# A planned delta-rule and mixture-of-experts layer: the experts' first products of the last three groups move to the projections' two PSUM banks, and the hand-over of the last chunks uses a second bank

## The chip, the core and the metric

The kernel runs on one core of a Trainium2 chip. The time is the device time of one execution in microseconds, and the figure given for a kernel is the median of its runs. A core has five engines that run beside each other, each with an instruction queue of its own that is worked through strictly in order: TensorE (PE, with its weight loads as PEld), VectorE (DVE), ScalarE (ACT), GpSimd (POOL) and SyncE (SP, which only issues transfers here). TensorE writes into PSUM, which is cut into eight banks of 512 fp32 words per partition. The kernel uses all eight.

## The reference

The input is `x` of shape (4, 1024, 128). All arithmetic is fp32. First comes an attention layer by the gated delta rule, then a layer norm; then a block with ordinary attention over the batch and a mixture of eight experts, then a layer norm. Cut to what matters:

```
# 1. delta rule: 16 heads of 8, causal over 1024 steps
q, k, v = silu(conv4(silu(x W + b)))          # q, k normalised per token over all 128 channels
a, b    = sigmoid(x Wa + ba), sigmoid(x Wb + bb)
S_t = a_t S_{t-1} - a_t b_t (S_{t-1} k_t) k_t^T + b_t v_t k_t^T
o_t = q_t S_t
x   = layernorm(x + o Wo + bo)
# 2. block: attention among the 4 places "t" of each token row, then experts
qkv = src @ in_proj_w.T + in_proj_b
x   = ln(src + softmax(q k) v @ out_w.T + out_b, ln1)
probs = softmax(tok @ gate_w.T + gate_b);  topv, topi = top_k(probs, 2)
for e in range(8):
    h = relu(tok @ w1[e].T + b1[e]) @ w2[e].T + b2[e]      # 128 -> 512 -> 128
    moe_out += combine[:, e:e+1] * h
x   = layernorm(x + ln(x + moe_out, ln2))
```

## The kernel before

The 1024 steps are cut into eight chunks of 128 (`NCHUNK`). Each chunk `c` goes through a fixed series of stages: `project` (inputs transposed, q, k, v and the two gates), `prepare` (convolution, the products k.k, a small triangular solve), `recur` (the recurrence, sixteen blocks of eight steps, each a multiply and a sum on VectorE twice over), `output` (what q reads from the states), `attend` and `attended` (the block's attention, layer norms, the gate and the ranks of the tokens), and then `experts`, which takes the chunks in the groups `(0, 1), (2, 3), (4, 5), (6,), (7,)`.

`experts` scatters every token twice into a buffer in HBM sorted by expert (L1555, an indirect transfer issued by POOL), reads it back in tiles of 128 rows, four at a time (`xl`), transposes them (L1571, bank `ph`), scales them on ScalarE (L1573, `xlT`), and then works tile by tile. One tile has one expert: its weights, 514 KB, are fetched by SP into one of three buffers `w_e` (L1586); four matmuls of 128x128 make the hidden layer in `ps_h` (L1596); four activations on ScalarE (L1605) add the bias and apply relu; four matmuls (L1609) make the result in the bank `pm`. A copy (L1617) and a transfer take four tiles to HBM (`ys`). When a group is done, POOL gathers each token's two rows (L1627), VectorE sums them, and two layer norms finish the chunk. There are 23 tiles in each group of two chunks and 15 in each group of one, 99 in all; in the text below they are counted 0 to 98, so that group (4, 5) has tiles 46 to 68, group (6,) tiles 69 to 83 and group (7,) tiles 84 to 98.

PSUM is handed out by tag, one bank for each buffer of a tag: `pa` has two banks (projections and convolutions), and `pk` (k.k), `su` (the states), `po` (output), `pc` (attend and attended), `ph` (transposed rows and hidden layer) and `pm` have one each. All instructions that touch one bank follow each other, whichever part of it they touch.

The order of the instructions is not the order of the program text. The program is recorded once; `forward` then plays it through with a list scheduler that has a table of costs (`price`), of delays between engines (`HOP`, row the waiting engine, column the one waited for), and of the transfers' rate; and `put_in_order` fixes the order that comes out, engine by engine. The rank of an instruction is the length of what follows it plus a number from `LEAD`: one row for each stage in the order of the text, one number for each sixty instructions of it. Where the plan leaves TensorE idle for more than `FILL_MIN`, `fillers` puts idle matmuls (L612, of the identity matrix) that keep its clock up; they write into whichever bank is free.

Of the kernel before, what the change touches and what calls it, by code (L numbers as in the profile page):

```python
# [84 lines left out]
class Slots:  # L85
# [33 lines left out]


HOP = (
    (0.0, 0.054, 0.053, 0.054, 0.05, 0.044),
    (0.038, 0.0, 0.033, 0.034, 0.04, 0.03),
    (0.037, 0.035, 0.0, 0.04, 0.04, 0.05),
    (0.09, 0.08, 0.063, 0.0, 0.06, 0.07),
    (0.031, 0.028, 0.026, 0.027, 0.0, 0.017),
)

OVERLAP = (0.0, 0.083, 0.11, 0.043, 0.0)

# [1 line left out]

PIECE = 60
LEAD = (
    (-596, -698,),
    (-695,),
    (1215, 1142,),
    (-239,),
    (-326,),
    (42, 327,),  # L140
    (-717, -154,),
    (-605, -1049,),
    (-810,),
    (-141, -914,),
    (-468,),
    (847, 645,),
    (142, 371,),
    (832, -867,),
    (-1488,),
    (-525, 14,),  # L150
    (21,),
    (154, 573,),
    (-536, 239,),
    (150, -335,),
    (-139, 302, 1084, 833, 618, 867, 306, -62, 535,),
    (-103,),
    (-319, 358,),
    (21,),
    (822, 1113,),
    (325, 133,),  # L160
    (-330, -211,),
    (-341,),
    (-499, -431,),
    (-273,),
    (809, 430,),
    (21, 79,),
    (510, -110,),
    (-99, 422, 15, 260, -43, 347, -211, 876, 125,),
    (-488,),
    (97, -532,),  # L170
    (-438,),
    (334, 1061,),
    (82, -55,),
    (-748, -468,),
    (-347,),
    (-566, -206,),
    (-890,),
    (673, 244,),
    (-525, -84,),
    (-74, -848,),  # L180
    (330, -102, -426, -699, -279, -40, -524, 453, 218,),
    (-566,),
    (129, -1199,),
    (-377, -137,),
    (-533, 514,),
    (378, 91, 339, 237, 165, 545,),
    (172,),
    (-80, 3,),
    (-409, -393, 106, 565, -698, 771,),
)  # L190
WINDOW, DOWN, UP = 3.413, 0.39, 0.77
FILL, FILL_MIN, FILLER = 0.7, 0.5, 0.225
TABLES = {"Silu": 1, "Sigmoid": 2, "Exp": 3}


# [221 lines left out]
def forward(units, rank):  # L417


    q = Queue(units, [u.preds for u in units], rank)  # L420
    begin_, end_ = [0.0] * len(units), [0.0] * len(units)
    order = [[] for _ in range(5)]
    size, cols, dma, pool, dve, table = None, [0.0] * 4, 0.0, 0.0, 0.0, 0
    slow, window, busy, carry, holes = True, 0, 0.0, 0.0, []
    for _ in units:
        now, e, k = q.take()
        u = units[k]
        begin = now
        if e == PE_:
            own, col = u.tile  # L430
            if size not in (None, own):
                begin = max(begin, max(cols)) + 0.1
            begin = max(begin, cols[col] if own[1] == 32 else max(cols))
            idle = max(cols + [q.free[e]])
            share = FILL * (begin - idle) if begin - idle > FILL_MIN else 0.0
            if share:
                holes.append((len(order[0]), idle, begin))
            spent = 0.0
            while True:
                t = idle + spent if share else begin  # L440
# [24 lines left out]
            end = begin + cost + u.long - u.cost  # L465
        elif u.bytes:
            dma = max(begin + u.cost + 0.2, dma) + u.bytes / 265e3
            end = dma + 1.4
            q.free[e] = begin + u.cost
        else:  # L470
            alone = u.kind in ("TensorTensor", "TensorScalarPtr", "TensorCopy")
            if e == DVE_ and alone and not any(u.psum):
                begin = max(begin, pool)
            if e == POOL_ and alone:
                begin = max(begin, dve)
            if e == ACT_ and u.table and u.table != table:
                begin += 1.28
                table = u.table
            end = begin + u.long
            q.free[e] = begin + u.cost  # L480
            if e == POOL_ and u.kind != "DMACopy":
                pool = end - 0.05
            if e == DVE_ and alone and not any(u.psum):
                dve = end - 0.05
        order[e].append(k)
        begin_[k], end_[k] = begin, end
        transfer = u.kind == "DMACopy"
        for s in u.succs:
            v = units[s]
            if v.engine != e or transfer:  # L490
                q.release(s, end + HOP[v.engine][5 if transfer else e])
            else:
                q.release(s, end if k in v.waits and e != PE_ else begin)
    return begin_, end_, order, holes


# [98 lines left out]
def delta_moe_kernel(  # L595
# [680 lines left out]
    def attend(c):  # L1276
# [25 lines left out]
        x1Tf = x1T.rearrange("p s t -> p (s t)")  # L1302

        def projected(i):
            ps = psum.tile([P, B, T], F32, tag="pc", name=f"ps_qkv{c}_{i}", bufs=1)
            nc.tensor.matmul(
                ps,
                lhsT=in_w[:, i * C : (i + 1) * C],
                rhs=x1Tf,
                start=True,  # L1310
                stop=True,
            )
            return ps
# [45 lines left out]
    def attended(c):  # L1359
# [1 line left out]
        x1, sc, v = scored.pop(c)  # L1361
        cxs = []
        for s in range(B):
            ps = psum.tile([P, B, T], F32, tag="pc", name=f"ps_a{c}_{s}", bufs=1)
            for f in range(2):
                nc.tensor.matmul(  # L1366
                    ps[:, :, f * T // 2 : (f + 1) * T // 2],
                    lhsT=spread[:, s, f],
                    rhs=sc,
                    start=True,  # L1370
                    stop=True,
                )
            cx = tile2k(f"cx{c}_{s}", "prod", 6)
            nc.vector.tensor_tensor(cx, ps, v, MUL)
            cxs.append(cx)
# [114 lines left out]
    def experts(group):  # L1490
# [71 lines left out]
        for i0 in range(0, nt, Q):  # L1562
# [18 lines left out]
            for i in range(m):  # L1581
                e = nc.sync.value_load(
                    expert_of[0:1, i0 + i : i0 + i + 1], min_val=0, max_val=E - 1
                )
                w = pl.tile([P, WP], F32, tag="w_e", name=f"w{g0}_{i0 + i}", bufs=3)
                nc.sync.dma_start(  # L1586
                    w, d["wp"][bass.ds(e, 1)].rearrange("o p f -> (o p) f")
                )
                w1 = w[:, 0:F]
                w2 = w[:, F : F + NF * C].rearrange("p (f c) -> p f c", f=NF)  # L1590
                b1 = w[:, F + NF * C : F + NF * C + NF]
                ps = psum.tile(
                    [P, NF, P], F32, tag="ph", name=f"ps_h{g0}_{i0 + i}", bufs=1
                )
                for f in range(NF):
                    nc.tensor.matmul(  # L1596
                        ps[:, f, :],
                        lhsT=w1[:, f * P : (f + 1) * P],
                        rhs=xlT[:, i, :],
                        start=True,  # L1600
                        stop=True,
                    )
                h = pl.tile([P, NF, P], F32, tag="h", name=f"h{g0}_{i0 + i}", bufs=2)
                for f in range(NF):
                    nc.scalar.activation(  # L1605
                        h[:, f, :], ps[:, f, :], AF.Relu, bias=b1[:, f : f + 1]
                    )
                for f in range(NF):
                    nc.tensor.matmul(  # L1609
                        ps_y[:, i, :],  # L1610
                        lhsT=h[:, f, :],
                        rhs=w2[:, f, :],
                        start=(f == 0),
                        stop=(f == NF - 1),
                    )
# [223 lines left out]
```

## Time and profile before

| | us |
|---|---|
| median of three runs (lowest, highest) | 833.56 (831.26, 834.96) |
| time of the profiled execution | 832.78 |
| its span, from the first instruction to the last | 831.1 |
| PE, DVE, POOL, ACT busy in the span | 699.4, 564.6, 475.4, 412.8 |
| last block of the last recurrence starts its last multiply | 565 |
| first matmul of tile 46, the first of group (4, 5) | 620.9 |
| last matmul of tile 98 | 802.5 |

A busy time is the sum of an engine's instructions in the one profiled execution. Matmuls overlap each other and their ends are modelled, so TensorE counts as busy for longer than the array works. The kernel has two halves with different limits: up to about 565 us the recurrence runs, and after it only what follows it is left. So shares over the whole span say little, and each part has to be read in its own stretch. Lines named below (L1596 and so on) are those of the kernel before.

### The profile page before, as it was taken

What the parts mean: (1) busy time and instruction counts of PE and PEld (TensorE: products, weight loads), DVE (VectorE), ACT (ScalarE), POOL (GpSimd) and SP (SyncE); (2) the same over time, 40 slices, a digit from 0 to 9 for tenths busy, and PEclk for the clock granted to TensorE, in tenths of its full rate; (3) what the DMA queues carried; (4) which work ended last, traced back from release to release, by engine and by line L of the source; (5) the groups of instructions that cost most, each with busy time, mean ns of one, the idle gap of its engine ahead of it and who ended that gap; (6) DMA issues with size and microseconds to landing.
All of it is one profiled execution on the core that took longest, in us unless ns stands there. A gap on an engine that the chain in (4) does not pass through costs nothing. (4 is left out here: it accounts for less than half of the span.)

```text
span 831.1 us, 15634 instructions
## 1 busy us (share of the span) xinstructions
PE 699.4 (84%) x5000; PEld 516.5 (62%) x5000; DVE 564.6 (68%) x1742; ACT 412.8 (50%) x1163; POOL 475.4 (57%) x656
## 2 busy tenths in 40 slices
PE   8989797889985988999889888799898999977750
PEld 5555545456553673667677577577477878777640
DVE  2167897898977998989899888987426351531303
ACT  5246362555653435486456435455325565465531
POOL 3534339849646748846746987653778621662213
PEclk9999999999997999999989999999899999999995
DMA  7642244252425245378458648568268688788741
GB/s 204 172 136 85 90 128 130 79 178 79 127 89 156 75 148 171 104 218 264 147 175 279 192 124 249 151 193 264 87 203 231 215 231 256 229 243 258 210 124 29
DMA packets 120070, 139.67 MB, mean 168 GB/s; under 512 B 9517, under 2 KB 90933, under 8 KB 119989
## 3 DMA queue, kind: packets, MB, share of 16 engines
q1 hardware_dynamic: 115893, 130.29, 52.0%
q0 software_dynamic: 4096, 8.40, 3.6%
q8 instruction: 39, 0.64, 0.3%
q14 instruction: 42, 0.34, 0.1%
HBM read 99.53 MB, written 39.12 MB: 167 GB/s over the span
## 5 line engine op out<-in xcount | busy, mean ns | idle before, releaser
L1605 ACT ACTIVATE h<-ps_ph,w_e 128x128 f32<-128x128 f32 x396 | 115.0, 368 | 91.2 <-PE ps_ph L1596 46.8
L1609 PE MATMUL ps_pm<-w_e,h 128*128 128x128 f32 x792 | 134.8, 296 | 19.9 <-ACT h L1605 18.6
L1609 PEld LDWEIGHTS ps_pm<-w_e,h 128*128 128x128 f32 x792 | 110.7, 193 | 39.8 <-ACT h L1605 34.9
L1596 PE MATMUL ps_ph<-xlT,w_e 128*128 128x128 f32 x792 | 116.8, 287 | 8.2 <-ACT xlT L1573 4.4
L1596 PEld LDWEIGHTS ps_ph<-xlT,w_e 128*128 128x128 f32 x792 | 101.1, 196 | 21.2 <-ACT xlT L1573 9.3
L897 PE MATMUL ps_pa<-z,diag 128*128 128x512 f32 x192 | 94.3, 620 | 7.8 <-ACT conv L906 3.0
L1627 POOL DMA_INDIRECT yg<-dr_ys,rows_at x64 | 62.2, 972 | 56.1 <-DMA dr_ys<-yl 26.9
L1555 POOL DMA_INDIRECT sorted<-x,rows_at x64 | 63.3, 989 | 49.9 <-DVE rows_at L1551 20.1
L1107 ACT ACTIVATE p<-ps_su,g_block 128x32 f32<-128x32 f32 x127 | 40.3, 317 | 98.4 <-DVE ps_su L1101 95.9
L1201 POOL TENSOR_TENSOR out_work<-sc__0_704,qg_r 128x512 f32<-128x512 f32 x64 | 73.4, 1165 | 14.3 <-PE ps_po L1205 5.7
L1633 DVE SCALAR_TENSOR_TENSOR acc<-yg,g2x,acc 128x128 f32<-128x128 f32 x64 | 24.0, 379 | 72.1 <-DMA yg<-dr_ys,rows_at 71.9
L1110 DVE TENSOR_TENSOR p<-ps_su,kd_r 128x256 f32<-128x256 f32 x127 | 53.1, 418 | 19.2 <-ACT p L1107 18.8
L897 PEld LDWEIGHTS ps_pa<-z,diag 128*128 128x128 f32 x192 | 33.9, 194 | 43.7 <-issue 30.3
L1101 DVE TENSOR_REDUCE ps_su<-z 128x32 f32<-128x288 f32 x128 | 58.1, 454 | 1.9
L1095 DVE TENSOR_TENSOR z<-ps_su,wt 128x256 f32<-128x256 f32 x128 | 53.4, 417 | 8.5 <-ACT su_out L1133 3.9
L1116 DVE TENSOR_REDUCE ps_su<-p 128x32 f32<-128x288 f32 x127 | 57.5, 453 | 1.6
L1173 POOL TENSOR_TENSOR out_work<-uc,q_r 128x192 f32<-128x192 f32 (+3 forms) x64 | 51.0, 827 | 12.3 <-DMA uc<-dr_su_back 11.8
L1219 POOL TENSOR_TENSOR out_work<-k_r,qu 128x128 f32<-128x128 f32 (+6 forms) x64 | 50.7, 818 | 7.8 <-DVE o L1227 5.3
L1086 ACT COPY z<-x 128x32 f32<-128x32 f32 x128 | 30.7, 245 | 38.7 <-DVE ps_su L1101 38.3
L940 POOL TENSOR_TENSOR work<-conv 128x320 f32<-128x320 f32 (+6 forms) x56 | 36.0, 666 | 22.4 <-DVE x L1035 19.5
L1035 DVE TENSOR_REDUCE x<-work 128x128 f32<-128x256 f32 (+6 forms) x56 | 45.5, 812 | 1.2 <-ACT work L1026 0.3
L1252 ACT ACTIVATE acc<-acc,le_nm,le_rs 128x128 f32<-128x128 f32 x64 | 28.1, 496 | 34.0 <-DVE le_nm L1250 34.0
(209 smaller groups left out, 1481.6 us busy)
## 6 DMA issues: line engine op xcount, KB each, us to landing
w_e<-in_wp SPq DMA_DIRECT2D x99, 514.0 KB, 4.7
dr_bounce<-conv SPq DMA_DIRECT2D x24, 256.0 KB, 2.4
xl<-sorted SPq DMA_DIRECT2D x21, 256.0 KB, 3.2
dr_ys<-yl SPq DMA_DIRECT2D x21, 256.0 KB, 5.0
kd_r<-dr_bounce SPq DMA_DIRECT2D x16, 256.0 KB, 3.1
work<-dr_bounce SPq DMA_DIRECT2D x16, 256.0 KB, 4.5
dr_su_back<-su_out SPq DMA_DIRECT2D x8, 512.0 KB
sorted<-yl SPq DMA_DIRECT2D x10, 256.0 KB, 4.3
```

Of the source, the lines that this page charges most:

```text
L897: nc.tensor.matmul(ps, lhsT=diag[:, i, j, :], rhs=z[:, i, :, j : j + T], start=(j == 0), stop=(j == KC - 1),)
L1095: nc.vector.tensor_tensor(z1n[:, :, :, 0:DH], s[:, :, None, :].to_broadcast([P, HD, J, DH]), wt[n // HALF][:, None, here_cut, :].to_broadc ...
L1101: nc.vector.tensor_reduce(u, z1n, AX.X, ADD)
L1110: nc.vector.tensor_tensor(p3[:, :, :, 0:J], u[:, :, None, :].to_broadcast([P, HD, DH, J]), ks[:, None, :, cut].to_broadcast([P, HD, DH, J] ...
L1116: nc.vector.tensor_reduce(ring[:, (n + 1) % (2 * RING), 0 : HD * DH].rearrange("p (d e) -> p d e", e=DH), p3, AX.X, ADD,)
L1173: gp.tensor_tensor(t[:, :, row_of(j) - r0 : row_of(j + 1) - r0], uv[:, :, 0 : j + 1], qv[:, :, j : j + 1].to_broadcast([P, BN, j + 1]), MUL,)
L1201: gp.tensor_tensor(t, sv[:, :, :, d_ : d_ + 1].to_broadcast([P, B, NB, J]), gv, MUL)
L1555: gp.indirect_dma_start(views[(i * 2 + g) * B + s][0 : nt * P, :], bass.IndirectOffsetOnAxis(ap=rows_at[:, g, s : s + 1], axis=0), x2[:, s ...
L1596: nc.tensor.matmul(ps[:, f, :], lhsT=w1[:, f * P : (f + 1) * P], rhs=xlT[:, i, :], start=True, stop=True,)
L1605: nc.scalar.activation(h[:, f, :], ps[:, f, :], AF.Relu, bias=b1[:, f : f + 1])
L1609: nc.tensor.matmul(ps_y[:, i, :], lhsT=h[:, f, :], rhs=w2[:, f, :], start=(f == 0), stop=(f == NF - 1),)
L1627: gp.indirect_dma_start(yg[:, s, :], None, ys[0 : nt * P, :], bass.IndirectOffsetOnAxis(ap=rows_at[:, g, s : s + 1], axis=0),)
```

## The change

Three sets of banks are changed. The hidden layers of the groups from chunk 4 on take turns in the two banks of `pa`, which no projection uses any more by then, instead of sharing the one bank `ph` with the transposes. For chunks 6 and 7 the products for v and q, and every second of the four products of attention, go to `pk`; the others stay in `pc`. The planner gets a longer delay from ScalarE to TensorE (0.053 to 0.1 us) and a table `SELF` of delays between instructions of one engine, and `LEAD` is replaced throughout, so that the order changes on every engine and in every stage.

```diff
 HOP = (
-    (0.0, 0.054, 0.053, 0.054, 0.05, 0.044),
+    (0.0, 0.054, 0.1, 0.054, 0.05, 0.044),
...
+SELF = (0.0, 0.034, 0.031, 0.05, 0.0)
...
 LEAD = (
-    (-596, -698,),
-    (-695,),
-    (1215, 1142,),
+    (-760, -1008,),
+    (-843,),
+    (1583, 1083,),
...
-                q.release(s, end if k in v.waits and e != PE_ else begin)
+                q.release(s, end + SELF[e] if k in v.waits and e != PE_ else begin)
...
         def projected(i):
-            ps = psum.tile([P, B, T], F32, tag="pc", name=f"ps_qkv{c}_{i}", bufs=1)
+            tag = "pk" if c >= 6 and i != 1 else "pc"
+            ps = psum.tile([P, B, T], F32, tag=tag, name=f"ps_qkv{c}_{i}", bufs=1)
...
         for s in range(B):
-            ps = psum.tile([P, B, T], F32, tag="pc", name=f"ps_a{c}_{s}", bufs=1)
+            tag = "pk" if c >= 6 and s % 2 else "pc"
+            ps = psum.tile([P, B, T], F32, tag=tag, name=f"ps_a{c}_{s}", bufs=1)
...
                 ps = psum.tile(
-                    [P, NF, P], F32, tag="ph", name=f"ps_h{g0}_{i0 + i}", bufs=1
+                    [P, NF, P],
+                    F32,
+                    tag="pa" if g0 >= 4 else "ph",
+                    name=f"ps_h{g0}_{i0 + i}",
+                    bufs=2 if g0 >= 4 else 1,
                 )
```

The arithmetic is the same. No instruction is added or removed but the idle matmuls, which the planner counts anew (343 before, 450 after), and one load of ScalarE's function tables, which the new order saves.

More of the change, by code (lines that the diff above doesn't have):

```diff
@@ L134 @@
 LEAD = (
-    (-596, -698,),
-    (-695,),
-    (1215, 1142,),
[L138 to L189, printed above, removed]
+    (-760, -1008,),
+    (-843,),
+    (1583, 1083,),
+    (-167,),
+    (-178,),
+    (160, 410,),
+    (-434, 63,),
+    (-563, -1111,),
+    (-331,),
+    (153, -935,),
+    (-165,),
+    (1003, 1356,),
+    (127, 57,),
+    (906, -869,),
+    (-2004,),
+    (-571, 203,),
+    (149,),
+    (639, 692,),
+    (-98, 183,),
+    (59, -429,),
+    (-365, 201, 808, 681, 347, 1338, 188, -115, 181,),
+    (-345,),
+    (-378, 116,),
+    (292,),
+    (1419, 1543,),
+    (571, 193,),
+    (-384, -274,),
+    (-193,),
+    (-1063, -14,),
+    (-387,),
+    (1251, 180,),
+    (-105, 87,),
+    (529, 38,),
+    (-156, 253, -100, 609, -81, 161, -584, 1175, 11,),
+    (-768,),
+    (-25, -836,),
+    (-16,),
+    (538, 1388,),
+    (455, 14,),
+    (-521, -939,),
+    (-724,),
+    (-334, 12,),
+    (-1129,),
+    (663, 550,),
+    (-89, -91,),
+    (111, -803,),
+    (-122, -187, -185, -699, -568, -188, -222, 160, 93,),
+    (-1086,),
+    (-231, -1273,),
+    (-85, 49,),
+    (-730, 376,),
+    (-335, -152, -76, 187, 92, 678,),
+    (135,),
+    (-98, 206,),
+    (-165, -723, -125, 425, -564, 836,),
 )
 WINDOW, DOWN, UP = 3.413, 0.39, 0.77
-FILL, FILL_MIN, FILLER = 0.7, 0.5, 0.225
+FILL, FILL_MIN, FILLER = .7, 0.5, 0.225
 TABLES = {"Silu": 1, "Sigmoid": 2, "Exp": 3}
```

## The prediction

> **What bounds the kernel now.** I read the page first, then the busy time by stretches, then the waits and the order of time inside the last stretches.
>
> ```profile
> PE 699.4 (84%) x5000; PEld 516.5 (62%) x5000; DVE 564.6 (68%) x1742; ACT 412.8 (50%) x1163; POOL 475.4 (57%) x656
> DVE  2167897898977998989899888987426351531303
> PEclk9999999999997999999989999999899999999995
> DMA  7642244252425245378458648568268688788741
> ...
> 500.00:565.00 65.00, 56.02 (x455) 44.94 (x453) 57.65 (x178) 36.30 (x119) 40.34 (x47) 0.97 0.69 208
> 565.00:621.00 56.00, 48.72 (x375) 36.40 (x375) 26.97 (x94) 19.08 (x55) 36.06 (x39) 0.94 0.60 177
> 621.00:701.00 80.00, 75.25 (x543) 65.59 (x544) 35.06 (x134) 45.48 (x135) 36.22 (x42) 0.98 0.78 230
> 701.00:752.00 51.00, 43.34 (x319) 38.17 (x318) 21.31 (x101) 29.75 (x88) 29.59 (x33) 1.00 0.81 237
> 752.00:803.00 51.00, 39.17 (x286) 34.78 (x284) 8.17 (x36) 26.94 (x81) 11.28 (x14) 1.00 0.72 215
> 803.00:831.00 28.00, 0.00 (x0) 0.00 (x0) 7.58 (x28) 3.33 (x9) 10.11 (x12) 0.57 0.13 35
> ```
>
> VectorE is eight to nine tenths busy up to 565 us, where the recurrence ends, and then falls off: the first part is VectorE's, and no bank of this change is used in it. After 565 us nothing is full. From 621 us on the 53 tiles of the last three groups run without a break to 802.5 us, 3.4 us each, with weight loads standing in 66 of 80 us, then 35 of 51. What they wait for, in 621 to 803 us, then the order of time at the end:
>
> ```profile
> PEld ps_pm L1609 <- ACT h L1605: 23.1, 40, 2.4
> PEld ps_ph L1596 <- ACT xlT L1573: 7.3, 11, 0.8
> PEld ps_ph L1596 <- DMA w_e<-in_wp: 2.9, 5, 0.9
> ...
> 797.23 1.09 PE L1596 MATMUL ps_ph<-xlT,w_e 128*128 128x128 f32 x8
> 798.41 1.14 ACT L1605 ACTIVATE h<-ps_ph,w_e 128x128 f32<-128x128 f32 x4 [1.30 <-issue]
> 798.83 1.00 PE L1609 MATMUL ps_pm<-w_e,h 128*128 128x128 f32 x6 [0.28 <-ACT h L1605]
> 799.67 1.09 PE L1596 MATMUL ps_ph<-xlT,w_e 128*128 128x128 f32 x8
> ...
> DMA to landing us min/median/max: 3.4/4.7/6.0
> ```
>
> The reader should see a ping-pong on one bank: hidden layer 1.1 us, relu 1.14 us, the next hidden layer only when the last relu has read the bank. That is 2.44 us from one tile to the next (797.23 to 799.67), the least there is. Every fourth tile the transposes and their scaling use the same bank, and the step is 3.7 to 4.0 us. The last row is the landing of a tile's weights after their issue.
>
> **The change, part by part.** The arithmetic stays; what moves is the waiting. I go by four stretches of the profiled execution (832.8 us, of which 1.7 lie outside the span; the median shown is 0.8 above it).
>
> Floors of a tile step first. TensorE: sixteen passes at the 0.112 us that separate neighbouring matmuls, and 0.11 for its share of the transposes: 1.9 us. ScalarE: 1.14 + (0.78 + 0.58) / 4 = 1.5 us. The weights, with three buffers: a fetch starts when the second matmuls three tiles back have ended, lands 4.7 us later, and then 1.1 (hidden layer) + 0.5 (first relu) + 1.3 (second matmuls) + 0.2 (hand-overs and issue) pass before the buffer is free: 7.8 / 3 = 2.6 us. This ring is not changed. So two banks can't bring a step under 2.6 us, and the plain step of 2.44 us, which lives on slack from slower ones, gains nothing. What gains is the fourth step (transposes and scaling can now go ahead in `ph`, 1.3 to 1.5 us) and each step in which ScalarE comes late for relu.
>
> *Tile 46 to the last of 68* (620.9 to 700.8 us: 80 us for 23 tiles, 3.48 each). TensorE also has chunk 7's attention here, so 66 us of weight loads are a floor. Six fourth steps at 1.3 make 7.8; I take 3.15 us a tile, 72.5 us: minus 7.5.
>
> *From there to tile 84* (700.8 to 751.9 us, 51.1 us). Before, group (6,)'s 15 tiles fill it, and group (7,)'s rows are ready early: its scatter ran from 719.7 to 729.7. In the order after, POOL has fifteen gathers of group (4, 5) ahead of that scatter instead of nine. So a second chain counts: copy 0.5, rows to HBM 5.0, fifteen gathers at 1.26 = 18.9, a layer norm's two instructions 1.3, eight scatters at 1.27 = 10.2, landing 4.8, read back 3.2, transposes and scaling 1.4: 45.3 us, whatever the tiles do. Fifteen tiles at 3.0 take 45. The order has sixteen idle matmuls with the transposes of tile 84, a hole in the plan, which says the same. I take 46: minus 5.
>
> *Tile 84 to the last matmul* (751.9 to 802.5 us, 50.6 us). No attention is left; 15 tiles at 2.95 and 1 us for the start: 45.3, minus 5.3. The gathers and norms of two chunks share ScalarE and the transfers here.
>
> *After it* (28.6 us: rows to HBM, eight gathers, two norms): the same instructions, 0.
>
> *Before tile 46.* The new leads move VectorE work of chunk 6's `attended` ahead of the last recurrence block: summed with the mean durations of the rows, 552.2 us instead of 546.5 stand before it. VectorE is 89% busy there, so up to 5.7 us later. On POOL eight scatters instead of three precede chunk 7's q.u products (five at 1.27 = 6.4 us later, if their ranks come as late as before: the first one waited 11.8 us for VectorE), but its eight gathers of group (2, 3) now follow that `output` (10.1 us sooner). I take plus 3.
>
> *Attention in two banks.* Four products of 0.45 us alternate with VectorE's 0.69 us; they started 2.0 us apart (682.4, 684.6, 686.6, 688.6) because tiles lie between. This shortens chunk 7's path by up to 4 x 0.5 us, plus 0.8 for v beside k's copy. The tiles fill those gaps on TensorE before, and chunk 7 becomes due only at tile 84, so 0; if chunk 7 is the late one, up to minus 3.
>
> *107 more idle matmuls*, 12 us in all at 0.112: 56 stand before tile 0 and 38 among the last three groups, all in holes planned at over 0.5 us. The clock row is already 9 nearly throughout, so I give them 0; where a hole is shorter than planned they delay TensorE, before tile 0 where VectorE is the bound, at the end by at most 38 x 0.112 = 4.3 us. `HOP` and `SELF` cost nothing themselves. The saved table load is 1.3 us of ScalarE in the first half, hidden by VectorE.
>
> Sum: -7.5 - 5 - 5.3 + 3 = -14.8. 832.8 - 14.8 = 818.0, and with the 0.8 to the median 818.8; I say 819.
>
> **Two rules weighed.** Against the change: the Trainium skill, "TensorE: Matmul & The Clock Gate", section "HAM oscillation — how this bites in real kernels", reports a matmul that waits for its operands' transfers, where a second PSUM buffer brought 126.6 to 125.5 us, nothing in effect. Scaled to the 181.6 us from tile 46 to 98 that is 1.6 us, and I would say 834. The rows differ from that case: only 2.9 us of the PEld waits are for weights and 30.4 for ScalarE behind the one bank. But the ring stands at 2.6 us, so once the bank is gone the rule's case begins. I take the trace as far as the ring. The other: "DMA: Bandwidth & Descriptors", "Specifications", gives about 358 GB/s of HBM for a core. A tile moves 514 KB and 128 KB of rows, 1.8 us by that rule. The trace's fullest stretch, 680 to 700 us, moved 267 GB/s at a share of 0.89, so 2.4 us a tile. By the rule transfers have room for my tile times; by the trace 2.95 us stays 20% clear of that, and a step much below 2.8 does not fit with the gathers beside it. I go by the trace.
>
> **Rivals.** *The ring takes what the bank gave* (no measurable change): the stall moves from "ps_pm <- ACT h" to "ps_ph <- DMA w_e". For it: the weights already land within 1 us of their use in many tiles, and a fuller DMA stretches 4.7 us to 5.5, which makes the ring 2.9 us and, with ScalarE's norms, 3.3 a tile. Gain in the three stretches 5, start plus 3: 831. Against: fourth steps are 1.3 us of TensorE and ScalarE alone.
>
> *The late first half* (slower): new leads everywhere let the last recurrence end later, and chunk 7's scatter waits behind six more gathers. Price: 5.7 (VectorE) + 6.4 (scatters first), and the middle stretch gives nothing since group (7,)'s rows come late; the first and last stretch give 5 together: plus 7, 840. It decides when tile 46 starts more than 13 us later. For it: VectorE has no room before 565 us, and an order fixed by a cost model is disturbed by anything the model doesn't know. Against: the eight gathers moved back, and total work is equal.
>
> *The plan comes true* (far faster): tile 46 is 6 us earlier since POOL is freed, steps reach 2.8 us, and chunk 7's two banks keep its rows in time: -6 - 15 - 8 = 804.
>
> *The change does not do what it says*: if the hidden layer still waited for relu, as with all four matmuls bound to one buffer, the step would stay at 2.44 and the fourth at 3.7. In the order after, first matmuls of a tile alternate one by one with second ones of the tile before, which one bank allows only once the last relu is through; so the banks do alternate. I hold it for 3 in 100 and count it to the ring's case.
>
> **Numbers.** My case 0.50 (807 to 828), the ring 0.15, late first half 0.28, plan comes true 0.07. A difference under 0.5%, 4.2 us, can't be told from none here. From the first case I put 0.02 within that, from the ring 0.02 to each side: faster 0.57, same 0.13, slower 0.30. The range leaves out the lower half of the fastest case and the worse half of the slower: 803 to 843.
>
> **What would show it.** Right: starts of tiles 46 to 98 about 3.0 us apart with no 3.7 us every fourth, "ps_pm <- ACT h" near halved from 23.1 us, "ps_ph <- DMA w_e" grown from 2.9, ten to twenty us from tile 46's start to the end gone, DMA near 250 GB/s there, tile 84 soon after its rows' scatter. Wrong: the last recurrence ends after 575 us, tile 46 starts after 630, or the steps stay at 3.4 with waits for weights.

## The result: 3.1% slower, with a first half that is 44 us later

The kernel after takes 860.6 us (median of 4 runs, 854.7 to 865.0), the kernel before 834.3 in the same comparison: a ratio of 1.031, interval 1.025 to 1.037. The profiled execution after took 862.9 us. From the page of the kernel after, and from its busy time by stretches:

```profile
PE 739.0 (86%) x5214; PEld 545.0 (63%) x5214; DVE 567.0 (66%) x1742; ACT 413.2 (48%) x1162; POOL 475.8 (55%) x656
DVE  2168798798784799779989988777546433442203
PEclk9999999799696999999999878899999999999995
...
657.00:732.00 75.00, 71.81 (x542) 62.71 (x540) 32.56 (x128) 45.76 (x136) 35.08 (x39) 1.00 0.87 263
732.00:784.00 52.00, 47.90 (x366) 44.05 (x365) 21.98 (x104) 28.96 (x88) 29.54 (x33) 0.97 0.81 252
784.00:833.00 49.00, 41.27 (x307) 37.87 (x304) 7.13 (x34) 25.19 (x79) 11.28 (x14) 0.97 0.66 200
```

VectorE does nearly the same work (567.0 us against 564.6), but its row falls off at 609 us instead of 565. The clock row has gaps in slices 8, 11, 13 and 23 to 26: summed from the trace, TensorE was granted half its clock for 89 us up to the recurrence's end, and for 44 us in the kernel before. From the recurrence's end on it takes 252 us, where the kernel before took 266. Stage by stage, in us from the start of the span:

| | before | after |
|---|---|---|
| last multiply of the last recurrence block ends ("recurrence's end" from here on) | 565.1 | 609.2 |
| first matmul of tile 46 | 620.9 | 657.3 |
| last matmul of tile 68 | 700.8 | 731.6 |
| transposes for tile 84 | 751.9 | 782.2 |
| last matmul of tile 98 | 802.5 | 832.7 |
| end of the span | 831.1 | 861.2 |

That last multiply (`z<-ps_su,wt`) and the VectorE instruction beside it, before and then after:

```profile
564.54 0.18 DVE L1415 TENSOR_REDUCE gm<-pb 128x4 f32<-128x32 f32 x1
564.67 0.42 DVE L1095 TENSOR_TENSOR z<-ps_su,wt 128x256 f32<-128x256 f32 x1
...
608.80 0.41 DVE L1097 TENSOR_TENSOR z<-ps_su,wt 128x256 f32<-128x256 f32 x1
609.13 0.14 DVE L1547 TENSOR_TENSOR rank<-rank,first 128x8 f32<-128x8 f32 x1
```

Before, the gate of chunk 5 has only begun by then (`gm` is the maximum for its softmax); after, the gate is done and the ranks nearly so.

The first half loses mostly in waits. From the start of the first recurrence to the end of the last, the two stretches read, before and after:

```profile
66.80:565.10 498.30, 433.26 (x3162) 304.18 (x3160) 442.46 (x1256) 259.45 (x747) 322.24 (x443) 0.96 0.50 152
...
66.60:609.20 542.60, 473.31 (x3331) 330.01 (x3330) 454.45 (x1279) 261.43 (x746) 320.69 (x442) 0.92 0.46 140
```

VectorE (the third number after the length) is busy 12 us longer, with 23 more instructions in the stretch, which are for the most part the gate and the ranks of chunk 5 done earlier, and idle for 88 us instead of 56. So of the 44 us some 12 are work moved ahead and some 32 are idle time. What it waited for in these stretches, before and then after:

```profile
DVE p L1110 <- ACT p L1107: 18.8, 40, 1.1
DVE prod L1374 <- PE ps_pc L1366: 4.4, 8, 1.6
DVE qu L1188 <- PE ps_po L1181: 1.7, 3, 1.0
...
DVE p L1112 <- ACT p L1109: 32.3, 55, 3.1
DVE prod L1378 <- PE ps_pc L1370: 9.4, 9, 2.0
DVE qu L1190 <- PE ps_po L1183: 6.2, 7, 1.8
DVE rank L1462 <- PE ps_pc L1460: 4.0, 2, 3.8
```

The reader should see that no large new wait has come (4.0 us for `rank` is the largest): waits for ScalarE's copy of the state and for TensorE have grown. How a block of the recurrence comes to be late is in the order of time after, in the last recurrence:

```profile
589.10 0.45 DVE L1118 TENSOR_REDUCE ps_su<-p 128x32 f32<-128x288 f32 x1
593.56 0.42 DVE L1097 TENSOR_TENSOR z<-ps_su,wt 128x256 f32<-128x256 f32 x1
594.02 0.46 DVE L1103 TENSOR_REDUCE ps_su<-z 128x32 f32<-128x288 f32 x1
594.94 1.65 ACT L1254 ACTIVATE x<-tmp,l_nm,l_rs 128x128 f32<-128x128 f32 x4 [0.43 <-DVE l_nm L1252]
596.49 0.86 ACT L1254 ACTIVATE acc<-acc,le_nm,le_rs 128x128 f32<-128x128 f32 x2
597.26 0.76 ACT L1272 ACTIVATE tmp<-ps_pc,ln 128x512 f32<-128x512 f32 x1
597.92 0.87 ACT L1254 ACTIVATE acc<-acc,le_nm,le_rs 128x128 f32<-128x128 f32 x2
598.69 0.30 ACT L1109 ACTIVATE p<-ps_su,g_block 128x32 f32<-128x32 f32 x1
598.82 0.69 DVE L1652 TENSOR_TENSOR acc<-acc,ln_g 128x512 f32<-128x512 f32 x1 [3.92 <-ACT acc L1254]
599.53 0.42 DVE L1112 TENSOR_TENSOR p<-ps_su,kd_r 128x256 f32<-128x256 f32 x1
```

The state is ready at 589.6 us (first line). Its next multiply (L1097) starts 4.0 us after that, behind other work in VectorE's own queue. The copy of the state on ScalarE (L1109, 0.30 us long) comes behind that multiply's sum, since both use the bank `su`. It could start at 594.5 us and starts at 598.7, behind the work of two layer norms in ScalarE's queue (594.9 to 598.8 us). Meanwhile VectorE's queue too stands still for 3.9 us on one of these norms, and the recurrence's product comes last. From the state to that product 10 us pass; the four VectorE instructions of a block are 1.8 us of work. This shows one case; that such cases account for all of the 44 us it does not show.

### The profile page after: what moved, and what is told of

It is laid out like the page before. It is cut to its first block, busy times and chain, and to the rows that moved or that the text cites. A ratio compares the mean times of both kernels' runs of the same rounds, so it can differ in the third digit from the quotient of the medians.

```text
span 861.2 us, 15975 instructions
## 1 busy us (share of the span) xinstructions
PE 739.0 (86%) x5214; PEld 545.0 (63%) x5214; DVE 567.0 (66%) x1742; ACT 413.2 (48%) x1162; POOL 475.8 (55%) x656
## 5 line engine op out<-in xcount | busy, mean ns | idle before, releaser
L1617 PE MATMUL ps_pm<-w_e,h 128*128 128x128 f32 x792 | 128.1, 292 | 12.9 <-ACT h L1613 11.3
L899 PE MATMUL ps_pa<-z,diag 128*128 128x512 f32 x192 | 102.5, 669 | 10.3 <-ACT conv L908 6.0
L1109 ACT ACTIVATE p<-ps_su,g_block 128x32 f32<-128x32 f32 x127 | 40.3, 317 | 115.6 <-DVE ps_su L1103 99.5
L1613 ACT ACTIVATE h<-ps_pa,w_e 128x128 f32<-128x128 f32 x212 | 60.3, 370 | 44.9 <-issue 23.2
L1613 ACT ACTIVATE h<-ps_ph,w_e 128x128 f32<-128x128 f32 x184 | 54.4, 369 | 44.5 <-issue 25.1
L1112 DVE TENSOR_TENSOR p<-ps_su,kd_r 128x256 f32<-128x256 f32 x127 | 53.4, 420 | 32.6 <-ACT p L1109 32.3
L899 PEld LDWEIGHTS ps_pa<-z,diag 128*128 128x128 f32 x192 | 37.0, 210 | 48.1 <-issue 34.0
L1604 PE MATMUL ps_pa<-xlT,w_e 128*128 128x128 f32 x424 | 64.7, 283 | 2.5 <-DMA w_e<-in_wp 2.4
L1175 POOL TENSOR_TENSOR out_work<-uc,q_r 128x192 f32<-128x192 f32 (+3 forms) x64 | 50.6, 823 | 28.7 <-DMA uc<-dr_su_back 21.0
L1097 DVE TENSOR_TENSOR z<-ps_su,wt 128x256 f32<-128x256 f32 x128 | 53.5, 418 | 10.5 <-ACT su_out L1135 6.0
L1604 PEld LDWEIGHTS ps_pa<-xlT,w_e 128*128 128x128 f32 x424 | 56.1, 197 | 5.0 <-DMA w_e<-in_wp 4.2
L1604 PE MATMUL ps_ph<-xlT,w_e 128*128 128x128 f32 x368 | 58.5, 292 | 0.3 <-DMA w_e<-in_wp 0.2
L1221 POOL TENSOR_TENSOR out_work<-k_r,qu 128x192 f32<-128x192 f32 (+6 forms) x64 | 50.6, 817 | 13.9 <-PE ps_po L1207 8.4
L1604 PEld LDWEIGHTS ps_ph<-xlT,w_e 128*128 128x128 f32 x368 | 49.6, 199 | 8.5 <-issue 4.2
L614 PEld LDWEIGHTS ps_ph<-ident 128*128 128x128 f32 x372 | 47.1, 201 | 5.6 <-issue 5.3
```

Of the source, the lines that this page charges most:

```text
L899: nc.tensor.matmul(ps, lhsT=diag[:, i, j, :], rhs=z[:, i, :, j : j + T], start=(j == 0), stop=(j == KC - 1),)
L1097: nc.vector.tensor_tensor(z1n[:, :, :, 0:DH], s[:, :, None, :].to_broadcast([P, HD, J, DH]), wt[n // HALF][:, None, here_cut, :].to_broadc ...
L1112: nc.vector.tensor_tensor(p3[:, :, :, 0:J], u[:, :, None, :].to_broadcast([P, HD, DH, J]), ks[:, None, :, cut].to_broadcast([P, HD, DH, J] ...
L1175: gp.tensor_tensor(t[:, :, row_of(j) - r0 : row_of(j + 1) - r0], uv[:, :, 0 : j + 1], qv[:, :, j : j + 1].to_broadcast([P, BN, j + 1]), MUL,)
L1604: nc.tensor.matmul(ps[:, f, :], lhsT=w1[:, f * P : (f + 1) * P], rhs=xlT[:, i, :], start=True, stop=True,)
L1613: nc.scalar.activation(h[:, f, :], ps[:, f, :], AF.Relu, bias=b1[:, f : f + 1])
```

## The experiments

Beside each kernel the kernel before ran on the same chip: 833.5 to 835.4 us on four chips, but 883.4 us on a fifth, where `splice`, `k101_hop`, `k101_self` and `pert_after` ran; there, only ratios and recurrence ends are read. The first two of these ran once more on another chip, as `splice2` and `k101_hop2`. Stage times are those of one profiled execution, which can lie off the median: by 4.8 us over it for `splice2` and 8.1 for `before_p_first`, by 4 to 10 us under it for `self_neg` (8.8), `after_p_first` (10.3), `pert_after` (7.3), `after_fill2` (4.4), `splice` (4.3) and `pert1` (4.0). All results, with the end of the last recurrence and the time from there to the end of the span, in us:

| kernel | leads | costs | banks | median | ratio, interval | recurrence's end | rest |
|---|---|---|---|---|---|---|---|
| before | old | old | old | 834.3 | | 565 | 266 |
| after | new | new | new | 860.6 | 1.031, 1.025 to 1.037 | 609 | 252 |
| `f_old_order` | order of before | | new | 836.6 | 1.002, 1.000 to 1.004 | 567 | 265 |
| `k100` | old | old | new | 843.5 | 1.012, 1.006 to 1.018 | 562 | 278 |
| `k010` | old | new | old | 860.3 | 1.030, 1.023 to 1.036 | 590 | 268 |
| `k001` | new | old | old | 859.3 | 1.025, 1.017 to 1.033 | 570 | 290 |
| `k101` | new | old | new | 836.8 | 1.004, 1.002 to 1.007 | 565 | 272 |
| `hyb_old_costs` | old, then new | old | new | 847.8 | 1.019, 1.012 to 1.026 | 578 | 270 |
| `after_fill2` | new | new | new | 881.0 | 1.063, 1.056 to 1.070 | 623 | 252 |
| `pert1` | old, noise | old | old | 867.7 | 1.046, 1.039 to 1.052 | 579 | 283 |
| `pert_after` | new, noise | new | new | 894.2 | 1.018, 1.010 to 1.026 | 584 | (301) |
| `k101_hop` | new | delay only | new | 869.8 | 0.984, 0.976 to 0.992 | 569 | (301) |
| `k101_hop2` | the same | | | 837.6 | 1.006, 1.002 to 1.010 | 565 | 269 |
| `k101_self` | new | SELF only | new | 898.7 | 1.020, 1.012 to 1.028 | 591 | (304) |
| `self_old` | old | SELF only | old | 852.4 | 1.024, 1.016 to 1.031 | 564 | 285 |
| `self_neg` | old | SELF reversed | old | 846.8 | 1.018, 1.014 to 1.022 | 566 | 271 |
| `splice` | both orders | | new | 868.0 | 0.988, 0.980 to 0.996 | 571 | (291) |
| `splice2` | the same | | | 835.8 | 0.999, 0.994 to 1.004 | 572 | 267 |
| `after_p_first` | new | new | new | 867.3 | 1.041, 1.033 to 1.048 | 601 | 255 |
| `before_p_first` | old | old | old | 841.1 | 1.006, 1.004 to 1.009 | 579 | 268 |

**The banks without a new order.** `f_old_order` makes the plan with the old banks (first `planned` below) and builds that order with the new ones (second).

```diff
-    try:
-        built(None)
-    except Planned as p:
-        nc = built(p.args)
...
+    order, _, times = planned()
+    order, fill, _ = planned(True, (order, times))
+    nc = built((order, fill), True)
```

> The order of the kernel before is kept instruction by instruction on every engine; only the three bank edits are made, and the idle matmuls are counted anew (371 instead of 343). Theory A (the new order of the first half is what costs; the banks are worth what the trace after shows from the end of the recurrence on): the recurrence ends at 565 us within 5, and the end comes 3 to 10 us sooner, 824 to 831 us. Rival B (the banks themselves cost time, by waits that the one bank did not have): 838 us or more with the recurrence's end unchanged. Rival C (the banks only pay with an order made for them): 832 to 836 us.

It came out level with the kernel before, 0.6 us above what rival C gave; A and B both miss. The waits of TensorE's weight loads from tile 46 on (621 to 804 us) say why:

```profile
PEld ps_pm L1621 <- ACT h L1617: 21.1, 39, 3.0
PEld ps_pa L1608 <- ACT xlT L1581: 4.3, 10, 0.8
PEld ps_ph L1579 <- DMA xl<-sorted: 2.7, 1, 2.7
PEld ps_pa L1608 <- DMA w_e<-in_wp: 1.6, 5, 0.5
```

Of 23.1 us behind relu, 21.1 remain: an order in which the next hidden layer stands behind three of the last tile's second matmuls waits for relu with any number of banks. Nor do the banks cost time of their own, or no more than 0.4%.

**One part alone, and two together.** `k100` has the banks, `k010` the costs, `k001` the leads, `k101` leads and banks; `hyb_old_costs` has the old leads up to `output` of chunk 6 and the new ones after it.

```diff
 k010, and nothing else:
-    (0.0, 0.054, 0.053, 0.054, 0.05, 0.044),
+    (0.0, 0.054, 0.1, 0.054, 0.05, 0.044),
+SELF = (0.0, 0.034, 0.031, 0.05, 0.0)
 hyb_old_costs, on new banks and old costs (in short: the kernel has the numbers):
-LEAD = NEW
+LEAD = OLD[:46] + NEW[46:]
```

> The bank edits with the old leads, the old delay table and no SELF; the planner orders anew. Theory A: the first half stays near the old order, 820 to 830 us. Rival D (the leads were fitted to one program so closely that any change of what the planner sees unsettles the order everywhere): the recurrence ends at 585 us or later and the time is 850 us or more.

> Only the planner's costs are new (0.1 instead of 0.053 us from ScalarE to TensorE, and SELF); leads and banks are old. Theory A, with the leads as the cause: 830 to 842 us. Rival E (the costs are the cause: the planner takes them for real): 850 us or more, with the recurrence's end 20 us or more later. Rival D says the same as E here, since the old leads meet costs they were not made for.

> Only the leads are new; costs and banks are old. Theory A: the recurrence ends 25 to 45 us later, as in the kernel after, and the time is 855 to 880 us, since the banks' gain is missing. Rival E: 830 to 845 us. Rival D: 850 us or more.

> New leads and new banks with the old planner costs. The kernel with new leads alone ended its recurrence at 570 us but needed 290 us from there; the kernel after ended it at 609 us and needed 252 us. Theory F (the costs cause the late first half, the leads fitted to two banks cause the short second half): recurrence's end 565 to 578 us, 252 to 262 us from there, 818 to 840 us. Theory D (any plan that the leads were not fitted to is worse by some per cent, whatever its parts): 850 us or more.

> New banks and old costs; the leads of all stages up to the output of chunk 6 are the old ones, those from the experts of chunks 4 and 5 on the new ones. Theory F: the first half as before (565 us within 5) and the second half as in the kernel after (252 to 262 us), 817 to 830 us, faster than both. Theory D: neither half keeps its time; 840 us or more, as with the banks alone under old leads (843.5).

`k100` keeps the first half and loses 12 us in the second, between what A and D said and in neither's range: from the recurrence's end to tile 46 it takes 74.4 us, where the kernel before takes 55.8, and from there to the last matmul of tile 98 174.7 us against 181.6. `k010` falls to E and D, `k001` to A and D by its time, though its first half is only 5 us late: the loss is in the second half. `k101` meets theory F (565 us), with 272 us from there instead of up to 262. So the new leads do belong to the new banks: with them 837, without them 859. What moves the kernel after from 837 to 861 is that the costs were changed too; and by themselves, on old leads and banks, the costs lose as much (`k010`). `hyb_old_costs`, which F wanted at 817 to 830, fails: half of one set of leads beside half of the other is no plan with the better half of each.

**Which of the costs.** `k101_hop` and its second run keep the delay of 0.1 us and set SELF to zero, `k101_self` the other way round; `self_old` puts SELF alone into the kernel before, and `self_neg` SELF with the sign turned.

```diff
 self_neg:
+SELF = (0.0, -0.034, -0.031, -0.05, 0.0)
```

> New leads and banks, of the new costs only the 0.1 us from ScalarE to TensorE; SELF is zero. New leads and banks took 836.8 us with the old costs and 860.6 with both new ones. If this delay is the cause: 852 us or more. If SELF is: 834 to 842. Theory D (any change of what the planner sees moves it off the point its leads were fitted to): 845 us or more here and in the run with SELF alone.

> New leads and banks, of the new costs only SELF; ScalarE to TensorE stays at 0.053. If SELF is the cause: 852 us or more. If the other is: 834 to 842. Theory D: 845 us or more in both.

> The kernel before with its own leads, banks and delays; only SELF is put in with the sign turned round (-0.034, -0.031, -0.05 us), a change of the same size as the one made, in the direction away from what the trace shows. Theory L (the delay itself makes the planner let the recurrence stand back): the recurrence ends at 560 to 572 us, as in all plans so far without SELF (562 to 579), and the time is 830 to 845 us. Theory D (what counts is only the distance from the plan the leads were tuned to): the recurrence ends at 580 us or later, 850 us or more.

> The kernel before with SELF alone (0.034, 0.031, 0.05 us). Theory L: the recurrence ends at 584 to 610 us, as in all five plans so far that have SELF, 850 to 870 us. If it was the pair of costs: below 580 us.

> New leads, new banks and the 0.1 us delay once more, for the same reason. On that chip it stood at 0.984 of the kernel before, with the recurrence's end at 569 us. If that carries over: 815 to 828 us. If it came from that chip alone: 832 us or more.

With the delay alone the time is 837.6, as without it. The 0.984 on the chip with 883 us did not carry over. With SELF on the new leads and banks the recurrence ends at 591 us. By then every plan with SELF had a late first half, and none without: theory L. `self_old` ends it: SELF alone, on old leads and banks, ends the recurrence at 564 us, and its 2.4% are lost in the second half. And `self_neg` loses 1.8%, with a recurrence that ends at 566 us in an execution 8.8 us under its median. A change of a few hundredths of a microsecond costs about as much in one direction as in the other. L falls. What SELF does depends on the rest of the plan: on new leads and banks SELF moves the recurrence's end (565 us with the delay alone, 591 with SELF alone, 609 with both), on the old ones SELF alone does not (564) and both do (590). The delay alone on the old leads was not run.

**The leads with noise.** `pert1` and `pert_after` add the same random numbers, with a spread of 20, to the leads of the kernel before and of the kernel after: one draw.

```diff
-    (-596, -698,),
-    (-695,),
-    (1215, 1142,),
+    (-570, -669,),
+    (-694,),
+    (1200, 1120,),
 ...
```

> The kernel before with its own banks and costs; each of its leads is changed by a random number with a spread of 20, where the leads run to over 1000. Theory D (the leads are a tuned point, and plans beside it are worse): 840 us or more. If plans are equally good around it: 830 to 838 us.

> The kernel after, each lead changed by a random number with a spread of 20, as was done to the kernel before, which lost 4.6% by it. If the kernel after is itself a tuned point on the chip: 880 us or more. Theory D, second part (it is no such point but one plan among many): 848 to 875 us, within 2% of its own 860.6, to either side.

The kernel before loses 4.6% by this noise, more than by the change in question, and in both halves. The kernel after with noise stands at 1.018 of the kernel before on its chip. Since that is the chip on which the second half was longer for all four kernels (291 to 304 us), it can't be set against 1.031; what can be read is the recurrence's end, 584 us with noise against 609 without. Its execution was 7.3 us under the median, which can't make up 25: the first half of the kernel after was not a point that noise spoils.

**The clock.** `after_fill2` keeps the order of the kernel after, with two idle matmuls for each one.

```diff
-        n = int(FILL * (until - idle) / FILLER)
+        n = int(2 * FILL * (until - idle) / FILLER)
```

> The kernel after, in its own order on every engine, with twice as many idle matmuls (949 instead of 450) in the same places. Theory G (half-clock time is what makes the first half late: 89 us of it up to the recurrence's end instead of 44): half-clock time falls below 60 us and the recurrence ends at 590 us or sooner, 830 to 848 us. Theory H (the order itself makes VectorE wait; the clock only follows from the idle time): half-clock time falls, and the recurrence's end stays within 6 us of 609; 856 us or more, since the idle matmuls also stand in the way.

Half clock up to the recurrence's end falls from 89 to 34 us, less than in the kernel before, and the recurrence ends 13 us later: against theory G, and later than theory H allowed (6 us). The page shows TensorE full and VectorE no better:

```profile
PE 800.5 (91%) x6212; PEld 633.7 (72%) x6212; DVE 564.3 (64%) x1742; ACT 413.9 (47%) x1162; POOL 475.3 (54%) x656
```

The run can't show what the clock alone would bring, since the idle matmuls stand in the way as well. But two other traces settle more. `k101`, from its first recurrence to its last, was granted hardly more clock than the kernel after (0.92), and its recurrence is not late:

```profile
66.50:564.50 498.00, 436.83 (x3091) 301.21 (x3093) 436.18 (x1244) 255.24 (x731) 318.23 (x435) 0.93 0.48 147
```

And `self_old` has 354 idle matmuls ahead of the recurrence's end at 564 us, the kernel after 371. So neither the lower clock nor the number of idle matmuls is enough to make the first half late.

**The first half of one, the second of the other.** `splice` and `splice2` are one kernel: what the plan of before starts by the end of the last recurrence keeps that order, the rest follows in the order of after.

```diff
+    for e, (a, b) in enumerate(zip(old, new)):
+        first = [k for k in a if t_old[0][k] <= cut]
+        have = set(first)
+        order.append(first + [k for k in b if k not in have])
```

> No new plan: every instruction that the kernel before places ahead of the end of the last recurrence keeps its order of before on every engine, and all others follow in the order of the kernel after, with its banks. Theory J (the two halves are independent: the second half of the kernel after is worth its 252 us after any first half): the recurrence ends at 566 us within 4, 818 to 826 us in all. Rival K (the second half of the kernel after was short because its first half, by being late, had already done work that belongs behind): 830 to 838 us, with the second half at 264 us or more.

> The spliced order once more, since its first runs fell on a chip on which the kernel before itself takes 883 us; its recurrence ended there at 571 us. Theory J: 252 to 258 us from the recurrence's end, 820 to 830 us in all. Theory K: 264 us or more from there, 832 us or more in all.

Rival K holds by its time: J's 830 us or less is out, and at 0.999 (0.994 to 1.004) the spliced order can't be told from the kernel before. After a first half of 572 us the order of after needs 267 us, not 252. The two rows from the recurrence's end on, `splice2` and then after:

```profile
572.20:838.90 266.70, 217.48 (x1588) 188.32 (x1588) 94.03 (x389) 123.35 (x365) 123.88 (x139) 0.90 0.65 197
...
609.20:861.20 252.00, 206.53 (x1564) 177.95 (x1562) 90.57 (x366) 123.06 (x364) 124.88 (x141) 0.94 0.67 206
```

The kernel after has 23 VectorE instructions fewer left to do there, the gate and ranks of chunk 5 that the rows of group (4, 5) wait for. The first tile of that group comes 48.1 us after the recurrence's end in the kernel after, 59.8 in `splice2`, 55.8 in the kernel before. The trace of `splice2` is 4.8 us over its median, with a lower clock in this part; with all of that taken off, 262 us are left. So of the 14 us that the kernel after regains behind the recurrence, some 10 are work that its longer first half had already done, and no gain of the second half.

**The recurrence's copy first on ScalarE.** `after_p_first` and `before_p_first` take the plan as it is and move the copy of the state ahead of every ScalarE instruction that is planned to start later than it could.

```diff
+        ready = max(end[p] + HOP[ACT_][units[p].engine] for p in u.preds)
...
+        while j and begin[queue[j - 1]] >= ready and queue[j - 1] not in u.preds:
+            j -= 1
...
+            queue.insert(j, queue.pop(i))
```

> The kernel after, its order kept but for one thing: on ScalarE the scaled copy of the state (L1109), for which the recurrence's next product on VectorE waits, goes ahead of every instruction that the plan starts later than that copy could start; 46 of the 127 copies move, by 81 places in all. VectorE waits 32.3 us for these copies in the first half of the kernel after, 18.8 in the kernel before. Theory M (the first half is late since short recurrence work stands behind long work in ScalarE's queue): this wait falls to 22 us or less and the recurrence ends at 600 us or sooner, 840 to 853 us. Rival N (where the queues stand still is set by what the planner can't foresee, so a repair by its own times does little): the wait stays above 28 us, the time within 1% of 860.6.

> The same edit on the kernel before (44 copies move, by 66 places). Theory M: the wait falls from 18.8 us to 14 or less and the time to 825 to 832 us. Rival N: 832 to 842 us.

Rival N on both. VectorE's largest row in the first half, in `after_p_first` and then in `before_p_first`:

```profile
DVE p L1132 <- ACT p L1129: 29.8, 51, 5.2
...
DVE p L1132 <- ACT p L1129: 22.4, 39, 3.0
```

The wait falls from 32.3 to 29.8 us in the first, in an execution 10.3 us under the median, and stands at 22.4 (18.8 before) in the second, 8.1 over its own. By their medians both kernels are no faster than without the edit. The plan's own times don't say where the queues will stand still, so this edit, which goes by them, doesn't help. A copy put first in ScalarE's queue whatever the plan's times was not run.

## Why the prediction was wrong, step by step

*The step that failed* is "before tile 46": plus 3 us forecast, plus 36.4 measured (620.9 to 657.3): 44.1 later at the recurrence's end, 7.7 of it regained. I had worked it out from what moves across the end of the last recurrence (5.7 us on VectorE, 6.4 and 10.1 on POOL) and took the rest of a wholly new order as neutral. But all 128 blocks of the recurrence lie in it, each with four VectorE instructions and a hand-over to ScalarE, in queues where anything late holds up what is behind. Counting moved instructions can't see that: the count gave 5.7 us for VectorE, where 12 us of work moved ahead (of chunk 5, not of chunk 6) and 32 us of idle time came with it. The new costs belong to this step as well: "`HOP` and `SELF` cost nothing themselves" passes over the order that the planner makes from them, and the runs put the late first half there (565 us with new leads and banks, 609 with the new costs besides). Why this plan makes the queues stand still longer stays open. My slower rival had the place right, the late first half, and drew its price from the same count: 12 us before tile 46 instead of 36.4. I also held equal work to be a reason against it; over the whole kernel VectorE's work was nearly equal (564.6 and 567.0 us), and its idle time in the first half was not (56 and 88).

*Tile 46 to the last of 68*: minus 7.5 forecast, minus 5.7 measured (74.3 us). The mechanism was right for the fourth steps: from the starts of the hidden layers in the traces, the step into a tile that begins a new set of four takes 4.1 us in the median before (3.7 to 8.5, not to 4.0 as I read it) and 2.9 after, over the twelve such steps behind tile 46 other than the one into tile 84. With one bank it stays (4.0 in `k001`), as with two banks in the old order (4.2 in `f_old_order`); with two banks and a plan made for them it falls (2.6 in `k100` too). In sum these twelve steps give 19.4 us, but the other 39 take 8.7 more, and the step into tile 84 takes 4.5 more. The waits of weight loads in the kernel after, 657 to 833 us:

```profile
PEld ps_pm L1617 <- ACT h L1613: 16.8, 32, 4.6
PEld ps_pa L1604 <- DMA w_e<-in_wp: 4.2, 9, 0.9
PEld ps_ph L1575 <- DMA xl<-sorted: 2.1, 2, 1.4
PEld ps_ph L1575 <- ACT xlT L1577: 1.0, 3, 0.4
...
DMA to landing us min/median/max: 3.4/4.5/6.4
```

The hidden layer no longer waits for the scaled rows (7.3 us before), behind relu there are 16.8 instead of 23.1, and waits for weights grew from 2.9 to 4.2. The weights landed as before, and transfers moved 263 GB/s over 75 us, close to the fullest stretch before (267 GB/s over 20 us).

*From there to tile 84*: minus 5 forecast, minus 0.5 measured (50.6 us). The second chain was the right one, but it took 50.6 us up to tile 84's transposes, not 43.9 (the 1.4 us for transposes and scaling lie behind them). The first gather starts 6.7 us after tile 68's last matmul, not 5.5, since POOL's queue has a layer norm ahead of it. Fifteen gathers and the two norm instructions took 22.6 us (738.4 to 761.0) instead of 20.2, since gathers wait for VectorE to free their buffer. From the scatter's end to the first transpose it took 10.7 us, not 8.0:

```profile
770.46 0.97 POOL L1559 DMA_INDIRECT sorted<-x,rows_at  x1 [0.30 <-issue]
...
773.43 2.33 SPq L1590 DMA_DIRECT2D w_e<-in_wp  x2
776.08 0.93 SPq L1570 DMA_DIRECT2D xl<-sorted  x2
...
778.55 3.07 PE L614 MATMUL ps_ph<-ident 128*128 128x128 f32 x26
782.15 0.66 PE L1575 MATMUL ps_ph<-ident,xl 128*128 128x128 f32 x4 [0.54 <-DMA xl<-sorted]
```

The time from issue to landing, of that scatter and then of that read:

```profile
DMA to landing us min/median/max: 4.2/4.2/4.2
...
DMA to landing us min/median/max: 5.3/5.3/5.3
```

The last scatter landed 4.2 us after its issue, at 774.6 us. The read of group (7,)'s rows stands in SP's queue behind two weight fetches, the second of which waits for a buffer until 775.4 us; that costs 1.5 us. The larger part is the read itself: issued at 776.1 us, it landed 5.3 us later and its transposes began after 6.1, where I had taken 3.2, the median over the kernel before. Against that, the scatter landed 3.2 us after POOL was done with it, not 4.8. The two weight fetches are under way at the same time; that they slow it is not shown.

*Tile 84 to the last matmul*: minus 5.3 forecast, 0 measured (50.6 us). One step, from tile 90 to 91, took 8.8 us; the longest in this stretch before was 5.7:

```profile
801.90 1.16 PE L1604 MATMUL ps_pa<-xlT,w_e 128*128 128x128 f32 x8
804.21 0.35 DVE L1641 SCALAR_TENSOR_TENSOR acc<-yg,g2x,acc 128x128 f32<-128x128 f32 x1 [4.12 <-DMA yg<-dr_ys,rows_at]
807.32 0.49 ACT L1254 ACTIVATE acc<-acc,le_nm,le_rs 128x128 f32<-128x128 f32 x1 [6.02 <-DVE le_nm L1252]
807.72 1.12 ACT L1613 ACTIVATE h<-ps_pa,w_e 128x128 f32<-128x128 f32 x4
808.12 1.54 PE L1617 MATMUL ps_pm<-w_e,h 128*128 128x128 f32 x8 [4.39 <-ACT h L1613]
```

Tile 90's hidden layer is done at 803.1 us. Its relu stands on ScalarE behind a norm of an earlier chunk, that one waits for its mean and variance from VectorE and POOL, and these for a gather that landed late. I had named the sharing of ScalarE by norms and priced it as their work; what it costs is their waiting. A second bank did nothing for that.

*The idle matmuls* were mis-sized: one fp32 matmul is two passes in the trace (the 450 of the order after are 900 rows of TensorE), so 107 are 24 us and not 12. In the same way a product of attention is 0.9 us (four rows), not 0.45. *The case against a second PSUM buffer* came nearer than my sum in its result for the banks alone: with the order kept they brought nothing (1.002), though not for the reason that I gave it, transfers, since waits for weights were 1.6 us and waits for relu stayed.

What the chances missed is that the kernel before looks like a tuned point and the change is a new plan. On the chips where the kernel before takes 833.5 to 835.4 us, fourteen other kernels ran, and none is faster. Two can't be told from it (`f_old_order`, `splice2`), three lose 0.4 to 0.6% (`k101`, `k101_hop2`, `before_p_first`), and eight lose 1.2 to 4.6%; the last, `after_fill2`, is the one with twice the idle matmuls. The kernel after, at 3.1%, lies among them. Why the order of before is better than its neighbours, these runs do not settle: it is not the clock, not the number of idle matmuls, not SELF, and not the copy's place in the plan of ScalarE's queue, each taken alone.

## What to carry to other kernels

When a change replaces numbers that steer a scheduler, its price is not the sum of the instructions it moves: make the new plan a case of its own, and take its spread from the old plan with noise in its numbers, which here, in one draw, gave 4.6% for a spread of 20 in numbers that run to over 1000. Test a buffer with the order kept, and then with a plan made for it: here it was worth nothing by itself, and with such a plan it shortened the steps that it was meant for while others grew. And where engines work queues in order, the cost of a neighbour in a queue is how long it waits as well as how long it runs.

## What the runs showed of the hardware

The same kernel took 833.5 to 835.4 us on four chips and 883.4 on a fifth. Two kernels ran there and on another chip: their first half was as long (569 and 571 us for `k101_hop` and `splice`, 565 and 572 on the other chip), and the part behind it 24 to 32 us longer; why, their traces do not show. In the traces before and after, a VectorE instruction that uses the result of the one ahead of it mostly starts 34 to 35 ns after that one's end, and a weight load that waited for ScalarE 51 to 52 ns, so that SELF was right for VectorE and the new 0.1 us too long; neither a right nor a wrong number made a better plan by itself. Twice the idle matmuls do hold the clock (0.97 granted over the first half instead of 0.92) without making anything earlier.
